# Moving a bookkeeping job of layers 0 and 1 into small parts behind named VectorE copies

## The chip, the cores and the metric

The kernel runs on one NeuronCore of a Trainium2 chip. Its engines each work through their own queue in order: TensorE (PE, matrix products), VectorE (DVE), ScalarE (ACT), GpSimd (POOL) and SyncE (SP, which mostly issues DMAs). The metric is the time of one execution on the device in microseconds.

## The reference

A graph network of four layers over 16 graphs (images, below) of 1024 nodes with 256 features, float32. Each layer adds to x what a graph layer makes of the normalised input:

```python
h = jnp.maximum(_layernorm(x), 0.0);  x = x + layer(h, adj, ...)
# layer 0: h' = h @ W.T + b;  u = adj * exp(e_i + f_j);  a = u / u.sum(2);   a @ h'
# layer 1: (d^-1/2 adj d^-1/2) @ (h @ weight) + bias, d = adj.sum(-1) + 1e-5
# layer 2: node after node, i = 0..1023:
#          x_par = (adj[:, i] / deg)^T h;  a GRU cell of (h_e[i], x_par) gives h[i]
# layer 3: agg = eps*h + adj @ h;  silu(rmsnorm(agg @ W1 + b1)) @ W2 + b2
```

Layer 2 is sequential over nodes. The kernel works it off in groups: within each block of 128 nodes it finds an order in which groups of 16 nodes don't depend on one another, as far as the edges (adj not zero) allow. That order is data, so it is computed in the kernel, by the function `orders`.

## The kernel before

Everything here happens in `layers_0_1` (L247 to L538), about the first 1500 us. A loop over i = 0 to 17 runs layer 0 of image i (`layer_0`) and then layer 1 of image i-1 (`layer_1`), with the preparation of image i+1 (`prepare`: statistics, q in L340, f in L342, then gs in L347) in between. A planner fixes the order of instructions on each engine when the program is built; data waits are added by it.

`sums` computes agg = adj @ h in four parts (two halves of 512 nodes by two halves of the features): eight matmuls each (L309) into one PSUM tile `pa` of two, then a copy to SBUF. Parts with c == 0 are copied by ScalarE (L312), those with c == 1 by VectorE (L314). So each layer of each image has two VectorE copies; counted from 0 over the whole stage, copies 4i-2 and 4i-1 belong to layer 0 of image i, and 4i and 4i+1 to layer 1 of image i-1. After sums come the matmuls with the weights (L379 in layer 0, L410 in layer 1), and pd (L361) takes gs of the next image.

`orders` holds two generators, advanced a part at a time by the loop:

- `places` (L126) reads pieces of adj (`piece`: eight DMAs at L113 and the comparison at L114, into a tile named "ad") and gives every node of a block its place: five small VectorE instructions a node (L135 to L140); then a rank is formed by comparing and reducing 16 columns at once (L149, L151), and a transposition on TensorE (L154). A part comes after each slot of `layer_0`.
- `rest` (L158) makes index tables: L162, 128 instructions, then writes of order_d (SP, L177) and reads of table (GpSimd, L181). It then reads adj again in eight pieces and finds how many rounds each group needs (L195, L196, then L201 to L236, transpositions L222). Its parts come in `layer_1` from i = 9 on, although the planner may place them earlier where nothing holds them.

From i = 9 (`ready`), `put_in_order` permutes what layer 2 will read, images 2k and 2k+1 in iteration 9 + k, image 14 in 16 and 15 in 17: it loads ad (SP, L423, L424), ab (L427) and mostly h (L430), scales ad on GpSimd (L435 to L440), permutes h by matmuls with a one-hot matrix `to` (L448, evacuated by L450 and L452), then ad (L461, L463, evacuated by L468 and L470), and multiplies (L476, L482).

The tiles named "ad" have one buffer together: the pieces of adj in `orders`, the tile `less` of the ranking, and the ad of `put_in_order` use it in turn. The tiles h2 have two buffers, shared by layer 1's output (ScalarE, L301) and by the h that `put_in_order` loads; x (loaded at L322) has three.

Of the kernel before, what the change touches and what calls it, by code (L numbers as in the profile page):

```python
# [2 lines left out]

# [6 lines left out]
F32 = mybir.dt.float32  # L10
AF = mybir.ActivationFunctionType
ALU = mybir.AluOpType
# [4 lines left out]
P = 128  # L17
# [4 lines left out]
S = 16  # L22
# [18 lines left out]
def gnn_stack(ctx: ExitStack, tc: tile.TileContext, a: dict, out: bass.AP):  # L41
# [65 lines left out]
    def orders(pool, psum):  # L107
# [9 lines left out]
        def tile_(name, n=P):  # L117
            return pool.tile([P, n], F32, name="o_" + name)
# [7 lines left out]
        def places():  # L126
            nc.vector.memset(bins, TOP)
            nc.vector.tensor_scalar(open_, step[:, :S], -1.0, TOP - 1, op0=ALU.mult, op1=ALU.add)
            nc.vector.tensor_scalar(below, open_, 1.0, None, op0=ALU.add)
            nc.vector.memset(held, 0.0)  # L130
            for j0 in range(0, P, S):
                nz = piece(j0, ALU.is_equal, 2 * TOP)
                for j in range(j0, j0 + S):
                    mine = bins[:, j : j + 1]
                    nc.vector.scalar_tensor_tensor(fit, below, mine, open_, op0=ALU.is_le, op1=ALU.mult)  # L135
                    nc.vector.tensor_reduce(mine, fit, AX.X, ALU.max)
                    nc.vector.scalar_tensor_tensor(held, open_, mine, held, op0=ALU.is_equal, op1=ALU.add)
                    nc.vector.scalar_tensor_tensor(open_, held, float(S), open_, op0=ALU.is_lt, op1=ALU.mult)
                    if j + 1 < P:
                        nc.vector.scalar_tensor_tensor(bins[:, j + 1 :], nz[:, j - j0, j + 1 :], mine, bins[:, j + 1 :],  # L140
                                                       op0=ALU.add, op1=ALU.min)
                    if j % 8 == 7:
                        yield

            key = tile_("key")
            nc.vector.scalar_tensor_tensor(key, bins, -256.0, step, op0=ALU.mult, op1=ALU.add)
            for i in range(0, P, S):
                less = pool.tile([P, S, P], F32, name="ad")
                nc.vector.tensor_tensor(less, key[:, None].to_broadcast([P, S, P]),  # L149
                                        key[:, i : i + S][:, :, None].to_broadcast([P, S, P]), ALU.is_lt)  # L150
                nc.vector.tensor_reduce(pos[:, i : i + S], less, AX.X, ALU.add)  # L151
                yield
            pt = psum.tile([P, 512], F32, name="pt")
            nc.tensor.transpose(pt[:, :P], pos, ident)  # L154
            nc.vector.tensor_copy(place, pt[:, :P])
            yield

        def rest():  # L158

            node = tile_("key")  # L160
            for p in range(P):
                nc.vector.scalar_tensor_tensor(junk, pos, float(p), step, op0=ALU.is_equal, op1=ALU.mult,  # L162
                                               accum_out=node[:, p : p + 1])
                if p % 32 == 31:
                    yield
# [17 lines left out]
            yield  # L183

            sub = tile_("sub")
            nc.vector.memset(sub, 0.0)
            for s in range(1, NS):
                nc.vector.scalar_tensor_tensor(sub, pos, float(s * S), sub, op0=ALU.is_ge, op1=ALU.add)
            chain = tile_("bins")
            nc.vector.memset(chain, 1.0)  # L190
            for j0 in range(0, P, S):
                nz = piece(j0, ALU.not_equal, 2.0)
                for j in range(j0, min(j0 + S, P - 1)):
                    row = nz[:, j - j0, j + 1 :]
                    nc.vector.scalar_tensor_tensor(row, sub[:, j + 1 :], sub[:, j : j + 1], row, op0=ALU.is_equal, op1=ALU.mult)  # L195
                    nc.vector.scalar_tensor_tensor(chain[:, j + 1 :], row, chain[:, j : j + 1], chain[:, j + 1 :],  # L196
                                                   op0=ALU.mult, op1=ALU.max)
                yield
            top = tile_("top", NS)
            for s in range(NS):  # L200
                nc.vector.scalar_tensor_tensor(junk, sub, float(s), chain, op0=ALU.is_equal, op1=ALU.mult)  # L201
                nc.vector.tensor_reduce(top[:, s : s + 1], junk, AX.X, ALU.max)
# [4 lines left out]
            for s, cuts in CUTS.items():  # L207
                for k, cut in enumerate(cuts):
                    if cut in cuts[:k]:
                        continue  # L210
                    nc.vector.tensor_scalar(junk, pos, float(s * S + cut), None, op0=ALU.is_lt)
                    nc.vector.scalar_tensor_tensor(junk, sub, float(s), junk, op0=ALU.is_equal, op1=ALU.mult)
                    nc.vector.scalar_tensor_tensor(junk, chain, 2.0 ** (k + 1), junk, op0=ALU.is_ge, op1=ALU.mult)
                    nc.vector.tensor_reduce(found, junk, AX.X, ALU.max)
                    nc.vector.tensor_tensor(early[:, s : s + 1], early[:, s : s + 1], found, ALU.max)
# [21 lines left out]
            yield  # L237
        return places(), rest()

# [7 lines left out]
    def layers_0_1():  # L247
        with ExitStack() as st:
# [46 lines left out]
            def normed(x, scale, mv, name, bufs):  # L295
# [6 lines left out]
                return h  # L302

            def sums(at, h, ag):

                def part(n0, c):
# [4 lines left out]
                    if c == 0:  # L311
                        nc.scalar.copy(ag[:, c, n0 : n0 + 512], pa)  # L312
                    else:
                        nc.vector.tensor_copy(ag[:, c, n0 : n0 + 512], pa)  # L314
                return [lambda n0=n0, c=c: part(n0, c) for n0 in (0, 512) for c in range(DC)]
# [39 lines left out]
            def layer_0(b, between):  # L355
# [9 lines left out]
                for part in sums(at[b], q[b], ag):  # L365
                    part()
                    if between:
                        between.pop(0)()
# [32 lines left out]
            def layer_1(b, between):  # L401
                ag = big.tile([P, DC, N], F32, name="ag", bufs=2)
                for part in sums(at[b], h1[b], ag):
                    part()
                    if between:
                        between.pop(0)()
# [85 lines left out]
            when.update({b + 2: (b,) for b in range(14, B)})  # L492
            parts_of_places, parts_of_rest = orders(big, psum)
            load(0)
# [3 lines left out]
            for i in range(B + 2):  # L498
                if i + 1 < B:
                    load(i + 1)  # L500
                jobs = []
                for b in when.get(i, ()):
# [12 lines left out]
                def slot():  # L515
                    for part in slots.pop(0):
                        part()
                    next(parts_of_places, None)
                if i < B:
# [6 lines left out]
                if 0 < i < B - 1:  # L526
# [3 lines left out]
                    between[1] = lambda: (load_half(i + 1), second())  # L530
                if i >= ready:
                    between += [lambda: None] * (4 - len(between))
                    for k in (1, 3):
                        between[k] = lambda part=between[k]: (part(), next(parts_of_rest, None))
                if 1 <= i <= B:
# [734 lines left out]
```

## Time and profile before

| | us |
|---|---|
| median of 3 runs | 4860.91 |
| lowest, highest | 4855.44, 4871.58 |
| the profiled execution | 4861.04 |
| its span | 4858.2 |
| PE busy | 4494.9 (93%) |
| DVE busy | 2303.1 (47%) |
| first copy L314 | starts at 41.77 |
| copy 20, copy 40, copy 63 | start at 457.34, 913.34, 1443.20 |
| first matmul of layer 2 (L749) | 1507.68 |

A line of a view of waits reads: engine, the instruction that waited, the one it waited for, and then us in total, times, and the longest. A line of a timeline reads: start and length in us, engine, line, operation, output and inputs with their sizes, the number of instructions put together, and in brackets the idle time of the engine before, with what ended it. PE matmuls are listed one record for each pass, two to an L309 instruction. Lines are those of the kernel before.

### The profile page before, as it was taken

To read this page: it belongs to the slowest core of one execution; us is meant where nothing else is said; L and a number is where in the kernel's file an instruction comes from. 1 tells how busy PE (TensorE), PEld (TensorE's weight loads), DVE (VectorE), ACT (ScalarE), POOL (GpSimd) and SP (SyncE) were. 2 spreads that over 40 slices of the span, in tenths; PEclk is the share of its full clock that TensorE was granted. 3 is DMA by queue.
4 is the path that set the end of the run, shared out by engine and by line. 5 is a ranking of instruction groups with operands and counts; after the bars stand their busy time and mean duration, and the time that the engine had idled before them with its cause. 6 is when DMAs were issued, how large, how long until landed. Compare 5 with 4: busy or idle time off the path is not lost. (4 is left out here: it accounts for less than half of the span.)

```text
span 4858.2 us, 52472 instructions
## 1 busy us (share of the span) xinstructions
PE 4494.9 (93%) x18199; PEld 3004.6 (62%) x18199; DVE 2303.1 (47%) x6354; ACT 1220.2 (25%) x2629; POOL 1586.6 (33%) x1939
## 2 busy tenths in 40 slices
PE   8998899999997999999999999998899999999999
PEld 4443455555555777777777777776455555555556
DVE  6667854455543444444444444454534344344342
ACT  1211112222212222222322222222223223223232
POOL 3223233343323322332232323331534234243231
PEclk9999999999998999999999999998899999999999
DMA  4333235555537444444344544420422231222100
GB/s 157 113 99 104 88 88 183 194 165 176 184 104 209 149 137 133 149 142 149 115 140 122 157 139 153 142 82 29 169 87 70 78 104 65 91 88 78 70 26 18
DMA packets 530978, 576.61 MB, mean 119 GB/s; under 512 B 42544, under 2 KB 439472, under 8 KB 528304
## 3 DMA queue, kind: packets, MB, share of 16 engines
q1 hardware_dynamic: 499536, 460.27, 30.6%
q0 software_dynamic: 31040, 111.44, 6.4%
q8 instruction: 197, 3.23, 0.3%
q14 instruction: 205, 1.68, 0.1%
HBM read 469.65 MB, written 116.65 MB: 121 GB/s over the span
## 5 line engine op out<-in xcount | busy, mean ns | idle before, releaser
L309 PE MATMUL pa<-at,h 128*128 128x512 f32 x1088 | 497.4, 610 | 32.9 <-DVE ag L314 32.9
L1145 PE MATMUL ph<-ag,w 128*128 128x512 f32 x1024 | 478.3, 609 | 32.7 <-DVE hh L1149 32.4
L1183 PE MATMUL po<-w,hh 128*128 128x256 f32 x2048 | 447.7, 379 | 0.0
L637 PE MATMUL pf<-hb,ab 128*128 128x256 f32 x1568 | 420.6, 387 | 29.0 <-DVE bxt L787 16.2
L1183 PEld LDWEIGHTS po<-w,hh 128*128 128x128 f32 x2048 | 387.8, 190 | 59.3 <-issue 7.9
L309 PE MATMUL pa<-at,q 128*128 128x512 f32 x960 | 424.2, 595 | 0.0
L309 PEld LDWEIGHTS pa<-at,h 128*128 128x128 f32 x1088 | 209.9, 196 | 278.5 <-issue 232.8
L749 PE MATMUL pf<-hs,wx 128*128 128x256 f32 x1536 | 351.1, 383 | 16.6 <-POOL hs L740 14.9
L1145 PEld LDWEIGHTS ph<-ag,w 128*128 128x128 f32 x1024 | 178.6, 189 | 294.0 <-DVE hh L1149 151.4
L1151 POOL TENSOR_TENSOR ss<-ss,sq 128x512 f32<-128x512 f32 x224 | 304.9, 1361 | 118.7 <-ACT sq L1148 114.3
L749 PEld LDWEIGHTS pf<-hs,wx 128*128 128x128 f32 x1536 | 292.1, 192 | 60.1 <-POOL hs L740 16.8
L637 PEld LDWEIGHTS pf<-hb,ab 128*128 128x128 f32 x1568 | 278.2, 192 | 69.5 <-DVE bxt L787 23.4
L309 PEld LDWEIGHTS pa<-at,q 128*128 128x128 f32 x960 | 178.2, 190 | 216.1 <-issue 212.6
L1149 DVE TENSOR_SCALAR hh<-ph,b 128x512 f32<-128x512 f32 x256 | 189.8, 746 | 153.8 <-ACT sq L1148 120.5
L784 PE MATMUL pf<-bd,h 128*128 128x384 f32 (+5 forms) x768 | 214.4, 373 | 51.7 <-DVE bxt L787 26.5
L1034 POOL DMA_INDIRECT hs_d<-h,table x128 | 129.3, 1010 | 365.4 <-ACT gates L757 179.7
L1130 PE MATMUL pa<-bxt,h 128*128 128x512 f32 x512 | 227.9, 597 | 18.6 <-POOL bxt L1112 18.6
L1130 PE MATMUL pa<-at,h 128*128 128x512 f32 x512 | 228.8, 597 | 0.0
L1148 ACT ACTIVATE sq<-ph,b 128x512 f32<-128x512 f32 x224 | 153.6, 686 | 233.6 <-PE ph L1145 188.2
L787 DVE TENSOR_TENSOR bxt<-bxt,pf 128x384 f32<-128x384 f32 (+5 forms) x384 | 141.2, 384 | 149.1 <-PE pf L784 146.6
L1175 ACT ACTIVATE hh<-hh,rw 128x512 f32<-128x512 f32 x256 | 168.4, 712 | 138.5 <-DVE hh L1174 136.5
L754 DVE TENSOR_TENSOR gates<-pf,bias 128x512 f32<-128x512 f32 x128 | 88.4, 691 | 227.3 <-PE pf L749 227.3
(253 smaller groups left out, 7318.6 us busy)
## 6 DMA issues: line engine op xcount, KB each, us to landing
at<-in_adjT SPq DMA_DIRECT2D x64, 1024.0 KB, 7.2
ab<-in_adj SPq DMA_DIRECT2D x128, 512.0 KB, 4.0
bxt<-in_adjT SPq DMA_DIRECT2D x64, 512.0 KB, 5.8
at<-in_adjT SPq DMA_DIRECT2D x64, 512.0 KB, 5.8
ad<-in_adj SPq DMA_DIRECT2D x128, 128.0 KB, 6.0
x_d<-x POOLq DMA_DIRECT2D x16, 1024.0 KB, 5.4
he_d<-h POOLq DMA_DIRECT2D x16, 1024.0 KB, 9.5
heT_d<-hT POOLq DMA_DIRECT2D x16, 1024.0 KB, 4.4
```

The lines of the kernel that those rows point to most:

```text
L309: nc.tensor.matmul(pa, h[:, mt, c * P : (c + 1) * P], at[n0 // 512][:, mt], start=mt == 0, stop=mt == NT - 1)
L637: nc.tensor.matmul(pb, ab[:, jts[k]], hb[:, jts[k]], start=k == 0, stop=k == len(jts) - 1)
L749: nc.tensor.matmul(pg[:, e], wx[:, c, q * D + e * P : q * D + (e + 1) * P], self.hs[:, c], start=c == 0, stop=c == DC - 1)
L784: nc.tensor.matmul(pf, h[:, g, c * P : (c + 1) * P], bd[:, g, b4 : b4 + 4, S : S + far], start=True, stop=True)
L787: return lambda: nc.vector.tensor_add(to, to, pf)
L1130: nc.tensor.matmul(pa, h[b][:, mt, c * P : (c + 1) * P], at[b][n0 // NH][:, mt], start=mt == 0, stop=mt == NT - 1)
L1145: nc.tensor.matmul(ph, w1[:, c, k * P : (k + 1) * P], ag[:, c, n0 : n0 + NH], start=c == 0, stop=c == DC - 1)
L1148: nc.scalar.activation(sq, ph, AF.Square, bias=b1[:, k : k + 1])
L1149: nc.vector.tensor_scalar(hh[:, k], ph, b1[:, k : k + 1], None, op0=ALU.add)
L1151: nc.gpsimd.tensor_tensor(ss, ss, sq, ALU.add)
L1175: nc.scalar.activation(hh[:, k], hh[:, k], AF.Silu, scale=rw[:, k : k + 1])
L1183: nc.tensor.matmul(po, hh[:, c, k * P : (k + 1) * P], w2[:, c], start=c == 0, stop=c == HC - 1)
```

## The change

`places` gives its parts after 4 nodes instead of 8, and ranks 8 columns at once instead of 16, so that L149 and L151 come 16 times at 1024 elements instead of 8 times at 2048. `rest` is split into `tables` (a part after 8 of its 128 instructions instead of 32) and `rounds` (a part after 8 nodes instead of 16; its array `chain` is now called `longest`, and the scratch tile of its end is one named "ad"). All rounds now come directly after all places.

The parts are taken in `layer_0` and `layer_1` after each of the four parts of sums, under `tc.issue_after`, which queues them on VectorE behind the last copy L314. Up to i = 8 these are parts of places and rounds, afterwards parts of tables; what is left of places and rounds at i = 9 is issued there at once. The hooks in `slot` and in `between` from i = 9 on are gone. What is computed stays the same.

```diff
-                    if j % 8 == 7:
+                    if j % 4 == 3:
                         yield
...
-            for i in range(0, P, S):
-                less = pool.tile([P, S, P], F32, name="ad")
-                nc.vector.tensor_tensor(less, key[:, None].to_broadcast([P, S, P]),
-                                        key[:, i : i + S][:, :, None].to_broadcast([P, S, P]), ALU.is_lt)
-                nc.vector.tensor_reduce(pos[:, i : i + S], less, AX.X, ALU.add)
+            yield
+            for i in range(0, P, 8):
+                less = pool.tile([P, 8, P], F32, name="ad")
+                nc.vector.tensor_tensor(less, key[:, None].to_broadcast([P, 8, P]),
+                                        key[:, i : i + 8][:, :, None].to_broadcast([P, 8, P]), ALU.is_lt)
+                nc.vector.tensor_reduce(pos[:, i : i + 8], less, AX.X, ALU.add)
                 yield
...
-        def rest():
+        def tables():
...
-                if p % 32 == 31:
+                if p % 8 == 7:
                     yield
...
+        def rounds():
+
             sub = tile_("sub")
...
-                yield
+                    if j % 8 == 7:
+                        yield
             top = tile_("top", NS)
+            junk = pool.tile([P, P], F32, name="ad")
...
-        return places(), rest()
+        return places(), tables(), rounds()
...
+            taken = []
+
+            def some_of(parts):
+
+                with tc.issue_after(taken[-1].ins):
+                    next(parts, None)
+
             def sums(at, h, ag):
...
-                        nc.vector.tensor_copy(ag[:, c, n0 : n0 + 512], pa)
+                        taken.append(nc.vector.tensor_copy(ag[:, c, n0 : n0 + 512], pa))
...
                 for part in sums(at[b], q[b], ag):
                     part()
+                    if taken:
+                        some_of(places if b < ready else tables)
...
                 for part in sums(at[b], h1[b], ag):
                     part()
+                    some_of(places if b + 1 < ready else tables)
...
-            parts_of_places, parts_of_rest = orders(big, psum)
+            places, tables, rounds = orders(big, psum)
+            places = chain(places, rounds)
...
+                if i == ready:
+                    for _ in places:
+                        pass
...
-                    next(parts_of_places, None)
...
-                if i >= ready:
-                    between += [lambda: None] * (4 - len(between))
-                    for k in (1, 3):
-                        between[k] = lambda part=between[k]: (part(), next(parts_of_rest, None))
```

## The prediction

> **What bounds the kernel now.** I read the page's head first, then the waits of TensorE over layers 0 and 1 (0 to 1470 us; layers 2 and 3 keep their instructions and order), then the timeline of each large wait.
>
> ```profile
> span 4858.2 us, 52472 instructions
> PE 4494.9 (93%) x18199; PEld 3004.6 (62%) x18199; DVE 2303.1 (47%) x6354; ACT 1220.2 (25%) x2629; POOL 1586.6 (33%) x1939
> ```
>
> TensorE is busy 93% of the span, so only its idle time and slowed stretches can be won or lost. Next, who made TensorE wait (us in total, times, longest):
>
> ```profile
> PE pa L309 <- DVE ag L314: 32.9, 12, 4.9
> PE pd L361 <- ACT gs L347: 25.3, 2, 17.4
> PE pmm L410 <- DVE x L411: 14.5, 5, 5.3
> ...
> PE pmm L379 <- DVE deg L375: 3.7, 1, 3.7
> ...
> PE pt L461 <- POOL ad L439: 3.1, 1, 3.1
> ```
>
> The first four trace back to VectorE, which serves the copies of sums late because orders' work stands ahead of them. The 17.4 us one, on VectorE and then on TensorE (start, us, instruction, idle before):
>
> ```profile
> 463.47 2.27 DVE L151 TENSOR_REDUCE o_pos<-ad 128x16 f32<-128x2048 f32 x1
> 465.67 0.34 DVE L340 TENSOR_SCALAR q<-x,mv 128x256 f32<-128x256 f32 x1
> 465.92 2.28 DVE L149 TENSOR_TENSOR ad<-o_key 128x2048 f32<-128x2048 f32 x1
> 468.13 0.94 DVE L342 SCALAR_TENSOR_TENSOR junk<-q,rs,v 128x256 f32<-128x256 f32 x1
> ```
>
> ```profile
> 466.74 1.89 PE L410 MATMUL pmm<-w,ag 128*128 128x256 f32 x8
> 486.07 1.94 PE L361 MATMUL pd<-at,gs 128*32 128x512 f32 x8 [17.44 <-ACT gs L347]
> ```
>
> Each L342 waits behind a compare and a reduction; the last ends at 485.6, so gs and pd come late. A later copy with no orders' work near it, on VectorE and then on TensorE:
>
> ```profile
> 650.42 0.17 DVE L350 TENSOR_TENSOR rg<-rs,gs 128x8 f32<-128x8 f32 x1 [0.37 <-ACT gs L347]
> 650.51 0.68 DVE L314 COPY ag<-pa 128x512 f32<-128x512 f32 x1
> ```
>
> ```profile
> 651.25 7.13 PE L309 MATMUL pa<-at,h 128*128 128x512 f32 x16 [1.44 <-DVE ag L314]
> ```
>
> Here the slack is already spent: eight L340 and L342 fill VectorE from 635.8, and this copy (number 28, counting L314 from 0) holds TensorE for 1.44 us. Whatever is put before it costs its full length.
>
> **What the Trainium skill says.** "TensorE: Matmul & The Clock Gate", its specification table: VectorE's queue is strictly first in, first out. The trace agrees: the copy at 650.51 starts as L350 is out of the way. The same page, Part 1 on the clock gate: an idle window of about 3.4 us drops TensorE to half rate until it has been busy for about as long. Agrees: after the 17.44 us wait, 26 records of L361 took 5.55 us against 2.95 elsewhere, 2.6 more. "VectorE: DVE Perf Modes", the TRN2 errata: a fixed cost per instruction with SBUF operands, 120 cycles beside one per element at 0.96 GHz. For 2048 elements that is 2.26 us, measured 2.28; for 1024, not in the trace of before, I estimate 1.19 us from that page. "Perfetto Trace Analysis", Optimizing Scalar/DVE Operations: breaking up instructions may let work finish sooner; the L342 chain above is such a case.
>
> **The change part by part.** Changes of TensorE's time, plus is slower. The order of instructions on each engine is fixed at build, and I compared it before and after. Up to copy 20 (first five iterations) it is practically the same: a piece of 16 nodes waits for the one ad buffer, not for its place in the queue. Gain there: 0.
>
> A, copies 20 to 27. A turn of the loop above is 463.47 to 469.00 = 5.53 us with one pair L149/L151. Halved blocks take out 2 x 1024 elements / 0.96 GHz = 2.13 us a turn, over five turns 10.7 us. The 128 L162 (pitch 0.334 us, 43 us at 504 to 550) leave this place; with them go waits that the window 457 to 580 and the next give as 7.5 (L309 on copies), 3.7 (deg) and 5.3 (L411), 16.5 together. New: eight half pairs beside later copies, 1.9, and the transpose L154 before copy 25, which waits for the last reduction, 2.8. Sum -22.5; with a little clock -23.
>
> B, rounds moved here from iterations 11 to 17. All pieces stand in a bunch of 31 or 32 L195/L196 right before copies 26, 28, 30 to 40, whatever the finer yields. Before 26 and 30 (in layer_0) VectorE has 7 us of other work in a 24.4 us interval of TensorE's sums and pd, so 8 us fit: 0 (8 each, were that cover gone). Before 28 and 32 the slack is spent: L114 0.7 + 31 x 0.246 (pitch measured for such rows) = 8.3, and for the shorter rows of copy 32 7.2. That is 15.5; two stalls over 3 us each cost 1.5 to 2.7 in the 16 records after them in the other stalls of before, I take 1.3 each since the second is partly absorbed: +18.
>
> C, copies 34 to 37. 48 L162 (16 us) and two pieces. The scheduler puts six of the eight L342 behind copy 36, so the copy is in time; the last copy of the iteration comes some 1.5 us late for L410, less small waits of images that no longer run there: +1. Cover: L342 behind the copy; without it about +8.
>
> D, copies 38 to 42. The pieces and `longest`'s junk hold the one ad buffer until the last L214, about 11 us after copy 40 (some 40 small VectorE instructions of 0.1 to 0.33 us). Only then can image 0's ad be loaded. In the trace of before a load issued at 949.92 is ready for TensorE at 960.9 (landing, L435 1.90, L440 1.68, L439 1.89): 11 us. TensorE meanwhile finishes its part some 4 us after that L214 and then waits about 7. Image 0's transposes take 7.9 us when nothing covers them (1457.4 to 1465.3). On SP, x of image 11 is queued behind image 1's ad, so it goes out about 21 us after image 0's load (11 + 7.9, and two issues) and lands 6.8 us later; statistics about 7, then L340/L342 at 1.6 us for eight: 13, then gs. pd comes 6 to 7 us late again. 7 + 6.5 + two uncovered image chains at 5 to 6 + clock 2.6 = 27, against 2 there before: +25 (10 to 40). Waiting with it on SP: the at loads of that iteration; on VectorE nothing.
>
> E, rest of iteration 11. Images 2 to 5 run in this iteration with one ad buffer: 11 + 7.5 = 18.6 us each, where their places on TensorE are about 15 apart: 3.5 late three times. 16 order_d writes (14 took 17.6 us on SP) and four table reads (2.77 us each on POOL) stand among their loads: mostly in the shadow of that ring. +8 (0 to 28).
>
> F, copies 46 to 61. Before, 357.9 us pass for 320 us of TensorE work at its own pace: 38 lost, 24.0 of it in named waits. In copies 33 to 45, images run without rounds and lose 14.4 in three iterations, 4.8 each. Four such: 19. -19, and a little for the ad buffer no longer shared with L113: -20.
>
> H, the end of layer 1. Before:
>
> ```profile
> 1476.78 3.50 PE L448 MATMUL pt<-to,h 128*128 128x128 f32 x16 [1.70 <-DVE to L432]
> 1481.25 0.44 PE L461 MATMUL pt<-to,ad 128*128 128x128 f32 x2 [0.96 <-POOL ad L439]
> ```
>
> Image 14's ad is loaded only at 1434.66, since L113's last piece held the buffer, and rounds' end stands among L411. From copy 63 (1443.2) to the first L749 (1507.68) are 64.5 us. With the ad buffer free and VectorE clear, L448 of image 15 can end 15.5 us after copy 63 and 25.7 us later comes L749: 41. Of the 23.5, 8.7 is image 14's TensorE work, done earlier and paid there: -15.
>
> Sum: -23 + 18 + 1 + 25 + 8 - 20 - 15 = -6. Span 4858.2 becomes 4852; the profiled run took 4861.04, 2.8 more than its span and level with the median 4860.91, so 4855.
>
> **The rivals.** Faster: the pile-up of D and E costs 8 instead of 33, because image 1's ad and x of image 11 go out while TensorE still has L410. For it: 15 us of other TensorE work lie there. Against: SP's fixed order. -31, so 4830. Decided by x of image 11 having landed within about 15 us of copy 41.
> Slower: SP. If the order_d writes (1.25 us each) delay the ad of images 2 and 3 by up to 20 us, E is 28, and x of image 11 late by 10 more makes D 35: -6 + 20 + 10 = +24, so 4885. For it: each write waits for an earlier transfer. Against: image 1's own chain covers the first eight. Over +0.3% from D + E = 54 on.
> Nothing: what is won up to copy 27 and after 46 is given back exactly by B to E; then 4861. The change doing nothing at all is excluded by the order from copy 20 on.
>
> **How the numbers follow.** 0.3%, 14.6 us, is about what a measurement can tell from no change: below 4846.3 is faster, above 4875.5 slower. The forecast with its own range 4841 to 4869: 0.40 (0.08 of it below 4846.3). Faster rival, 4815 to 4841: 0.28. Slower rival, 4876 to 4900: 0.28. Nothing: 0.04. So faster 0.36, same 0.36, slower 0.28. 4826 to 4890 leaves out about 0.08 and 0.10.
>
> **What would show it.** Right: the 17.4 us wait for gs falls to about 7 and the waits for deg and L411 at 500 to 600 go; L309 waits 9 to 10 us for copies 28 and 32; one group of waits of 20 to 30 us around copies 41 to 43, for ad on POOL and for gs; few waits afterwards; the first L749 some 41 us after copy 63. Wrong: VectorE serves copies 28 and 32 before the bunch (B is 0), or TensorE's idle time at images 0 to 5 is under 10 or over 55 us.

## The result and the profile after

The changed kernel is slower: 4887.26 us, median of 7 runs (4879.17 to 4894.69), against 4863.79 for the kernel before (7 runs, 4855.44 to 4871.58). The ratio is 1.0048, with a 95% interval of 1.0035 to 1.0062. The profiled run took 4883.2 us. Its page begins so:

```profile
span 4881.2 us, 52487 instructions
PE 4501.9 (92%) x18199; PEld 3001.2 (61%) x18199; DVE 2292.3 (47%) x6370; ACT 1219.6 (25%) x2629; POOL 1578.9 (32%) x1939
```

The span is 23.0 us longer, and TensorE's busy time 7.0 us longer with as many instructions. Lines of the kernel after lie 13 to 16 below those of the kernel before: L309 is L322, L314 is L327, L361 is L374, L410 is L426, L448, L461 and L468 are L464, L477 and L484. The view of waits of TensorE, layers 0 and 1 (us in total, times, longest):

```profile
PE pa L322 <- DVE ag L327: 43.4, 12, 9.4
PE pd L374 <- ACT gs L360: 20.3, 3, 8.5
PE pt L477 <- ACT hT L484: 14.8, 8, 6.9
PE pt L477 <- POOL ad L455: 10.6, 2, 8.3
PE pt L464 <- ACT hT L466: 9.5, 2, 6.6
...
PE pmm L426 <- DVE x L427: 7.5, 3, 3.6
```

The waits for x (L411 before, 14.5) and deg (3.7) have shrunk or gone, as the prediction has it. The waits for copies (32.9 before) have grown. Three groups weren't among the large ones: waits of `put_in_order` for hT and for ad.

To see where time went I compared the starts of the VectorE copies L314/L327, counted as in the text above, and took off the time that TensorE's instructions between two of them need (those of the layers by their place in the program, those of `put_in_order` by when they ran) at their clean pace in the trace of before (0.867 us for an L309, 0.432 for an L379 or L410, 0.2275 for an L361, 0.215 for an L371, 0.109 for a transposition, 0.434 and 0.11 for L476 and L482). What is left is lost, by waits or by a slower TensorE. The two kernels don't put the same work of `put_in_order` into a stretch, which this takes out. The stretch from copy 61 to 63, left out here, is -0.2 to 5.2 throughout. In us, in the order in which the kernels come below:

| lost between copies | 0–19 | 19–27 | 27–33 | 33–37 | 37–45 | 45–61 | 63 to layer 2 | layer 2 starts | from there to the end |
|---|---|---|---|---|---|---|---|---|---|
| before | 31.5 | 44.2 | 4.0 | 5.7 | 8.7 | 38.0 | 41.8 | 1507.7 | 3350.5 |
| after | 32.0 | 24.2 | 22.5 | 7.3 | 66.6 | 18.2 | 30.4 | 1534.2 | 3347.0 |
| `halves` | 31.5 | 32.2 | 16.2 | 5.6 | 8.9 | 37.0 | 41.2 | 1505.8 | 3355.0 |
| `halves_sp` | 33.1 | 39.4 | 2.3 | 5.7 | 9.0 | 34.4 | 42.8 | 1499.6 | 3346.3 |
| `rounds_odd` | 30.7 | 21.7 | 8.7 | 4.9 | 87.1 | 18.2 | 30.2 | 1535.0 | 3347.8 |
| `old_rounds` | 32.2 | 22.8 | 2.8 | 5.5 | 45.4 | 44.9 | 39.1 | 1529.1 | 3356.9 |
| `tables_late` | 33.3 | 24.4 | 22.6 | 7.6 | 43.5 | 53.7 | 28.4 | 1545.9 | 3356.4 |
| `three` | 32.2 | 24.1 | 22.5 | 7.3 | 52.1 | 15.4 | 30.0 | 1516.0 | 3338.9 |
| `three_late` | 31.8 | 23.2 | 22.3 | 7.6 | 15.8 | 68.7 | 30.9 | 1533.3 | 3349.2 |
| `tables_sp` | 31.9 | 23.3 | 22.2 | 7.3 | 60.2 | 17.5 | 30.1 | 1525.3 | 3349.6 |
| `three_sp` | 32.2 | 24.1 | 22.5 | 7.3 | 47.3 | 19.1 | 29.7 | 1514.9 | 3337.8 |
| `heT_h2` | 31.2 | 24.0 | 22.5 | 7.3 | 86.7 | 24.5 | 25.5 | 1554.7 | 3358.9 |
| `best2` | 32.3 | 22.6 | 11.9 | 37.3 | 13.0 | 17.0 | 29.0 | 1501.2 | 3345.3 |
| `best3` | 30.3 | 23.8 | 13.2 | 5.1 | 14.8 | 16.8 | 28.8 | 1471.5 | 3352.5 |

After against before: -20.0 from 19 to 27, +18.5 to copy 33, +57.9 from 37 to 45, -19.8 to 61, -11.4 at the end. Layer 2 starts 26.5 later, and 3.5 of that comes back in layers 2 and 3. The loss of 57.9 sits in one place: some 44 us of after's are lost between copies 41 (905.40) and 42 (996.04), all in iteration 11, where images 0 to 5 go through `put_in_order`.

On TensorE the two first stretches look as foretold. Its timeline: the wait for gs halved, the copies 28 and 32 late.

```profile
474.03 6.31 PE L374 MATMUL pd<-at,gs 128*32 128x512 f32 x26 [8.47 <-ACT gs L360]
...
637.85 9.84 PE L322 MATMUL pa<-at,h 128*128 128x512 f32 x16 [9.38 <-DVE ag L327]
...
722.67 10.09 PE L322 MATMUL pa<-at,h 128*128 128x512 f32 x16 [7.50 <-DVE ag L327]
```

The wait for copy 28 was 1.44 us before, and its 16 records then took 7.13. On VectorE the bunch of rounds stands directly ahead of the copy:

```profile
636.89 0.31 DVE L200 SCALAR_TENSOR_TENSOR o_bins<-ad,o_bins 128x97 f32<-128x97 f32 x1
637.12 0.68 DVE L327 COPY ag<-pa 128x512 f32<-128x512 f32 x1
```

The surprise is iteration 11. TensorE's timeline from copy 41 to copy 42, the records with the largest idle time ahead of them:

```profile
932.33 0.47 PE L477 MATMUL pt<-to,ad 128*128 128x128 f32 x1 [6.90 <-ACT hT L484]
...
944.51 3.62 PE L374 MATMUL pd<-at,gs 128*32 128x512 f32 x10 [4.32 <-ACT gs L360]
...
961.63 0.48 PE L477 MATMUL pt<-to,ad 128*128 128x128 f32 x1 [8.33 <-POOL ad L455]
...
988.10 1.97 PE L464 MATMUL pt<-to,h 128*128 128x128 f32 x8 [6.62 <-ACT hT L466]
```

Four stalls, 26.2 us, with TensorE slowed in between: the view by windows gives it a granted clock of 0.80 from 912 to 1005 us, where the whole span has 0.976. What the third stall waits for stands on GpSimd:

```profile
942.24 2.78 POOL L183 DMA_DIRECT2D table<-order_d  x1
945.48 0.57 POOL L501 DMA_DIRECT2D base_d<-bo  x1 [0.47 <-DVE bo L500]
953.94 2.77 POOL L183 DMA_DIRECT2D table<-order_d  x1 [7.89 <-issue]
956.72 1.10 POOL L451 TENSOR_SCALAR_AFFINE_SELECT ad<-ad 128x1024 f32<-128x1024 f32 x1
...
959.68 1.89 POOL L455 TENSOR_TENSOR ad<-ad,dinv 128x1024 f32<-128x1024 f32 x1
```

The ad of image 2 was issued on SP at 934.15, when image 1's last transposition out of that one buffer had just ended (933.67 and 0.42 us), so the order_d writes ahead of it on SP did not hold it up. By the 11 us from issue to ready that step D takes from the trace of before, TensorE could have had it at 945; it has it at 961.6. Behind the first table read GpSimd still sends a write of base_d, at 945.48. Then it does nothing for 7.89 us that the profile explains ("issue") until the second read begins, and ad's scaling stands behind that one. A table read has a record of 2.78 us, but it lands much later:

```profile
DMA to landing us min/median/max: 9.2/10.0/11.3
```

The first read landed 11.3 us after its start, at 953.5, and the second begins at 953.94. The third begins at 963.82 and landed after 9.2 us, at 973.0, and the fourth begins at 973.37. So what a read holds up is the next read, and with it all that stands behind that next read; other instructions follow a read at once, as L451 does here. In `tables_sp`, below, where SP issues the reads, the same scaling begins at 946.66. The writes of heT_d, near_d and next_d stand among the third and fourth read. The tile hT has one buffer, which an image uses twice, for its permuted h and then for its permuted ad, and each of these writes must have landed before TensorE's next transpositions can be put into it. The fourth stall is of this kind: near_d and next_d went out behind the fourth read, at 976.12 and 977.00, and landed after 9.8 and 10.4 us, at 985.9 and 987.4; near_d's of the two images before had taken 6.3 and 5.0.

The trace of before has the same in it, though nothing urgent stood behind it. GpSimd's timeline of before:

```profile
591.70 2.80 POOL L181 DMA_DIRECT2D table<-order_d  x1
602.15 2.75 POOL L181 DMA_DIRECT2D table<-order_d  x1 [7.65 <-issue]
604.89 0.89 POOL L417 DMA_DIRECT2D he_d<-h  x1
612.17 2.76 POOL L181 DMA_DIRECT2D table<-order_d  x1 [6.39 <-issue]
621.61 2.75 POOL L181 DMA_DIRECT2D table<-order_d  x1 [6.68 <-issue]
```

Starts are 9.4 to 10.5 us apart, and the write of he_d (L417) follows the second read at once. The first read landed 10.0 us after its start and the third after 9.1, and the read behind each began 0.3 to 0.4 us later. So four reads in a row take up GpSimd's queue for some 33 us, not 11. rs (L83) behind them was wanted only at 631.99.

The theory for the experiments is this. The 25 us by which D and E together were too small come from the table reads, of which each holds up the next one, and what stands behind that, for about 10 us just where six images need the queue; or, as a rival, from the six images alone, caught up in a row on one ad buffer and one hT buffer, with the rounds' late end in front. A second rival has the rounds themselves as the cause, through B and through when they end.

### The profile page after: what moved, and what is told of

Same layout as the page of the kernel before. It is cut to its first block, busy times and chain, and to the rows that moved or that the text cites. A ratio compares the mean times of both kernels' runs of the same rounds, so it can differ in the third digit from the quotient of the medians.

```text
span 4881.2 us, 52487 instructions
## 1 busy us (share of the span) xinstructions
PE 4501.9 (92%) x18199; PEld 3001.2 (61%) x18199; DVE 2292.3 (47%) x6370; ACT 1219.6 (25%) x2629; POOL 1578.9 (32%) x1939
## 5 line engine op out<-in xcount | busy, mean ns | idle before, releaser
L322 PE MATMUL pa<-at,h 128*128 128x512 f32 x1088 | 503.1, 615 | 43.4 <-DVE ag L327 43.4
L1160 PE MATMUL ph<-ag,w 128*128 128x512 f32 x1024 | 479.3, 610 | 32.3 <-DVE hh L1164 32.1
L322 PE MATMUL pa<-at,q 128*128 128x512 f32 x960 | 428.1, 597 | 0.0
L322 PEld LDWEIGHTS pa<-at,h 128*128 128x128 f32 x1088 | 211.9, 198 | 291.6 <-issue 235.1
L322 PEld LDWEIGHTS pa<-at,q 128*128 128x128 f32 x960 | 178.6, 191 | 213.5 <-issue 209.1
L799 PE MATMUL pf<-bd,h 128*128 128x384 f32 (+5 forms) x768 | 213.5, 372 | 49.5 <-DVE bxt L802 26.5
L1145 PE MATMUL pa<-bxt,h 128*128 128x512 f32 x512 | 227.5, 596 | 18.5 <-POOL bxt L1127 18.5
```

Source lines behind the costliest of these rows:

```text
L322: nc.tensor.matmul(pa, h[:, mt, c * P : (c + 1) * P], at[n0 // 512][:, mt], start=mt == 0, stop=mt == NT - 1)
L799: nc.tensor.matmul(pf, h[:, g, c * P : (c + 1) * P], bd[:, g, b4 : b4 + 4, S : S + far], start=True, stop=True)
L1145: nc.tensor.matmul(pa, h[b][:, mt, c * P : (c + 1) * P], at[b][n0 // NH][:, mt], start=mt == 0, stop=mt == NT - 1)
L1160: nc.tensor.matmul(ph, w1[:, c, k * P : (k + 1) * P], ag[:, c, n0 : n0 + NH], start=c == 0, stop=c == DC - 1)
```

## The experiments

**The smaller comparisons alone.** `halves` changes the kernel before in one place:

```diff
-            for i in range(0, P, S):
-                less = pool.tile([P, S, P], F32, name="ad")
...
+            for i in range(0, P, 8):
+                less = pool.tile([P, 8, P], F32, name="ad")
...
```

> The kernel before with nothing changed but the ranking in sixteen compares and reductions of 1024 elements. My theory of step A: five turns of the loop get 2.13 us shorter, so the wait for gs falls from 17.4 to about 7 us and the time by 10 us, to about 4853; the waits for deg and L411 stay, since the 128 table instructions stay where they are. Rival: the wait was for the whole backlog, and only moves to the next copy: no change, 4863.

4862.32 us against 4860.47 for before, ratio 0.9998 (0.9989 to 1.0007). Step A's first part is real: the stretch 19 to 27 loses 32.2 instead of 44.2, and the wait for gs falls from 17.44 to 8.5 us. But 27 to 33 loses 16.2 instead of 4.0. TensorE's waits there, 580 to 720 us:

```profile
PE pa L309 <- ACT ag L312: 7.0, 1, 7.0
PE pa L309 <- DVE ag L314: 4.2, 1, 4.2
```

The last table read starts 3.9 us later than in the kernel before, while TensorE is 12 us ahead, and this time rs, which is soon wanted, is behind the reads. GpSimd, and then VectorE, which waits for rs with its copies queued behind:

```profile
625.50 2.75 POOL L181 DMA_DIRECT2D table<-order_d  x1 [6.57 <-issue]
...
629.89 1.63 POOL L83 TENSOR_TENSOR rs<-rs_v,mhalf 128x8 f32<-128x8 f32 x1
```

```profile
631.55 0.17 DVE L396 TENSOR_TENSOR rd<-rs,dis 128x8 f32<-128x8 f32 x1 [12.65 <-POOL rs L83]
```

The gain of 12.0 us was given back, 12.2, in the next stretch. The time is the rival's, 4863, but not for the rival's reason, since the wait for gs did not move to the next copy. `halves_sp` adds one edit, the table reads issued by SP:

```diff
-                        nc.gpsimd.dma_start(table[k][:, g].rearrange("p t s -> p (t s)"),
+                        nc.sync.dma_start(table[k][:, g].rearrange("p t s -> p (t s)"),
```

> The kernel before with the sixteen half compares and the table reads issued by SP. In the half-compare kernel the stretch of copies 19 to 27 got 12 us shorter and that of 27 to 33 got 12.2 longer, with an rs on GpSimd 12.65 us late behind the table reads. Theory: with these on SP the 12 us stay won: 4848 to 4852. Rival: VectorE's table instructions, now later, cost the 12 us: 4862.

4852.67 against 4860.38, ratio 0.9982 (0.9973 to 0.9991), just above the range that was expected. The stretch 27 to 33 is back at 2.3, so it was the reads' hold on GpSimd that had taken the gain of `halves`. Layer 2 starts 8.1 us earlier than in the kernel before. But up to copy 27 only 4.8 of the 12.0 is left. On SP the second eight order_d writes now stand behind two reads, and VectorE waits for them, with copy 27 queued behind:

```profile
612.88 0.17 DVE L186 MEMSET o_sub<- 128x128 f32 x1 [14.84 <-DMA order_d<-o_sub]
```

In `halves` this wait is 6.07 us. Copy 27 starts at 615.25 instead of 606.81, and TensorE waits 4.61 us for deg behind it, where `halves` has no wait for deg. So the reads hold up SP too. The second edit was not run alone.

**Rounds.** `rounds_odd` lets the parts of rounds in the kernel after follow only the second and third part of sums, so that none is bunched ahead of the second copy of a layer:

```diff
+                    if b + 1 >= ready or not in_rounds or n in (1, 2):
...
+                    if taken and (b >= ready or not in_rounds or n in (1, 2)):
...
```

> The changed kernel, but parts of rounds are taken only behind the second and third part of sums, so that a piece stands before an odd copy (27, 29, 31, 33), where VectorE has nothing else. Theory (step B): the waits of 9.4 and 7.5 us for copies 28 and 32 go, with their slowed records 19 us, and the rest stays: 4868. Rival: VectorE's total work in these iterations binds, and the same 19 us are lost at other copies: 4887.

4886.59 against 4860.47, ratio 1.0058 (1.004 to 1.0076): no better than after. The time is the rival's, 4887, but the loss is not at other copies of these iterations. B itself goes as it should. From 27 to 33, 8.7 is lost instead of 22.5, and TensorE's waits for these copies, 16.9 us in after, are

```profile
PE pa L325 <- DVE ag L330: 4.9, 2, 3.5
```

But 37 to 45 loses 87.1, 20.5 more than in after. There, 880 to 1090 us:

```profile
PE pt L481 <- ACT hT L488: 24.5, 5, 13.0
PE pt L502 <- DVE hT L490: 7.9, 1, 7.9
```

The third and fourth table read now start at 952.52 and 962.26, and a write of heT_d is issued behind them at 966.70. hT can't be written before it has landed, and the wait of 13.0 us ends at 975.24. So what B costs and what iteration 11 costs are not independent: a gain before it shifts which instruction is behind a read.

`old_rounds` is the reverse: in the kernel after, rounds are given back their place in iterations 11 on.

```diff
-                    if j % 8 == 7:
+                    if j % 16 == 15:
...
-            places = chain(places, rounds)
...
+                if i >= 11:
+                    between += [lambda: None] * (4 - len(between))
+                    for k in (1, 3):
+                        between[k] = lambda part=between[k]: (part(), next(rounds, None))
```

> The changed kernel with places and tables as it has them, but rounds taken two parts an iteration in layer 1 from iteration 11 on, about where the kernel before has them, so that images start in iteration 9, two at a time. If tables alone, among images in iterations 9 to 11, cost what they seemed to (23 us of the 58): between copies 37 and 45 some 30 us are lost, against 8.7 before and 66.6 in the changed kernel, copies 19 to 33 lose 28 (24 and 4), and the time is 4855 to 4870. If rounds in front of the images are the cause of the whole: under 15 us are lost there, 4840 to 4852.

4883.71 against 4862.61, ratio 1.0043 (1.0033 to 1.0052). Without any rounds before it, and with images spaced as before, 37 to 45 still loses 45.4, where before loses 8.7. That is more than either expectation, 30 or under 15, and the time is above both ranges. What is left of the change in these iterations is the tables: their VectorE instructions, the order_d writes and the reads. TensorE's waits from 770 to 1000, and on GpSimd why:

```profile
PE pt L464 <- ACT hT L466: 15.7, 1, 15.7
PE pt L477 <- ACT hT L484: 13.7, 2, 13.1
```

```profile
929.50 2.75 POOL L183 DMA_DIRECT2D table<-order_d  x1 [8.53 <-issue]
...
933.12 0.57 POOL L470 DMA_DIRECT2D heT_d<-hT  x1
```

The read before it stands at 918.16. heT_d goes out 15 us after that, and TensorE's L477 at 944.24 has waited 13.12 us for hT. So rounds in front of the images are not the cause of the whole: 36.7 of the 57.9 us stay without them. And this is F too: with rounds put back, 45 to 61 loses 44.9 instead of 18.2.

**Reads and images, two by two.** In `tables_late`, tables are not made until i is 12. In `three`, six images are not caught up in one iteration: three are taken in each of the iterations 11 to 14. `three_late` has both edits.

```diff
-                        some_of(places if b < ready else tables)
+                        some_of(places if b < ready else tables if b >= 12 else iter(()))
...
-                    some_of(places if b + 1 < ready else tables)
+                    some_of(places if b + 1 < ready else tables if b + 1 >= 12 else iter(()))
```

```diff
-            when = {ready + k: (2 * k, 2 * k + 1) for k in range(7)}
-            when.update({b + 2: (b,) for b in range(14, B)})
+            when = {11 + k: (3 * k, 3 * k + 1, 3 * k + 2) for k in range(4)}
+            when.update({15: (12, 13), 16: (14,), 17: (15,)})
```

> The changed kernel, but tables are taken from iteration 12 on, so that the order_d writes on SP and the table reads on GpSimd are out of iteration 11. If they cause the pile-up there: the wait of 8.3 us for the scaled ad of image 2 and some 5 us behind it go, 4870 to 4875. If the six images in a row cause it by themselves: 4882 to 4890. The table instructions then stand among later images and may cost up to 5 us there in both.

> The changed kernel, but the images are put in order three at a time from iteration 11 on (0 to 2 in 11, 3 to 5 in 12, and so on; 12 and 13 in 15, 14 and 15 as before), so that none waits for rounds to end. If the six images that are caught up in one iteration are the cause: of the 58 us lost more than before between copies 37 and 45 at least 30 go, 4850 to 4860. If the late release of the ad buffer is, by delaying x of image 11: about the same as the changed kernel, 4880 to 4890.

> The changed kernel with images three at a time from iteration 11 and tables from iteration 12: what the late end of rounds costs with neither tables nor six images beside it. Between copies 37 and 45, where the changed kernel loses 66.6 us, the one with images in threes 52.1 and the one with late tables 43.5: if the causes are separate, 25 to 32 us; if images in threes only help because tables are there, 40 to 45. Later the tables cost some 30 us among images, as in the other run with late tables, so the whole is 4870 to 4890.

`tables_late` took 4896.08 against 4860.47, ratio 1.007 (1.0048 to 1.0092); `three` 4857.63 against 4860.47, 0.9998 (0.9987 to 1.001); `three_late` 4882.16 against 4862.61, 1.004 (1.0024 to 1.0055). Lost from copy 37 to 45:

| | tables in iteration 11 | tables later |
|---|---|---|
| six images in iteration 11 | 66.6 (after) | 43.5 |
| three images in iteration 11 | 52.1 | 15.8 |

So the tables as a whole (VectorE instructions, order_d writes and reads) cost 23.1 us beside six images and 36.3 beside three; six images instead of three cost 27.7 without the tables and 14.5 with them. The two overlap: 66.6 is less than 15.8 + 36.3 + 27.7 = 79.8. `three` met its time, 4850 to 4860, but with 14.5 us of the 30 that were expected in this stretch; `tables_late` came out slower than both its ranges, and `three_late` lost less than the 25 to 32 expected. With neither, 15.8 is left, 7.1 above the kernel before. What waits there is the end of rounds, from 854 to 1045 us:

```profile
PE pt L228 <- DVE o_top L208: 6.6, 1, 6.6
PE pt L464 <- ACT hT L466: 2.3, 2, 1.1
```

Moving the tables later doesn't take their price away. `tables_late` loses 53.7 in the stretch 45 to 61, 35.5 more than after, and `three_late` 68.7 there. In `tables_late`, 1060 to 1450 us:

```profile
PE pt L477 <- ACT hT L484: 15.9, 5, 13.2
PE pt L464 <- ACT hT L466: 15.1, 1, 15.1
```

Wherever the reads stand among images of `put_in_order`, hT's writes are behind them.

**The reads on another queue.** `tables_sp` is the kernel after with the edit of `halves_sp`, and `three_sp` is `three` with it.

> The changed kernel, but the four table reads are issued by SP instead of GpSimd, so that nothing on GpSimd stands behind them. Theory: of the 58 us lost between copies 37 and 45 beyond before, the 23 that tables cost there come from GpSimd standing still for the order_d writes, with the scaling of ad and the rs of the normalisation behind it; then 12 to 20 us go, 4867 to 4875. Rival: the DMA transfers themselves or SP's issues cost it: 4882 to 4890.

> The changed kernel with images three at a time from iteration 11 and the table reads on SP. If both causes are separate, their gains add: the 28 us of the one and 12 to 20 of the other, 4838 to 4848. If both remove the same wait: 4855 to 4860.

`tables_sp` took 4876.24 against 4860.38, ratio 1.0029 (1.002 to 1.0038), some 10 us better than after and between the two expectations; `three_sp` 4856.2, ratio 0.9991 (0.9983 to 0.9998), hardly better than `three` and in the range expected if both edits remove the same wait. From copy 37 to 45 `tables_sp` loses 60.2 instead of 66.6, `three_sp` 47.3 instead of 52.1. The Trainium skill says on the page "DMA: Bandwidth & Descriptors", in "Issuing engines are not separate DMA queues", that DMAs of all engines run on the same 16 DMA engines and that issuing from several only saves time on the sequencer. These runs agree that the choice of engine doesn't make most of the cost go: the longest wait of `tables_sp` from 885 to 1000 us is

```profile
PE pt L477 <- POOL ad L455: 13.9, 1, 13.9
```

since ad's load stands on SP, behind the reads (issued at 971.41, right after the second pair). The choice mainly says who is held. In `halves_sp`, where only order_d writes stood behind the reads on SP, layer 2 starts 6.2 us earlier than in `halves`.

**hT's buffer.** `heT_h2` writes heT_d from h2 instead of hT, so that hT comes free earlier. Layer 2 reads other values in this kernel.

```diff
-                        nc.gpsimd.dma_start(heT_d[b], hT)
+                        nc.gpsimd.dma_start(heT_d[b], h2[b].rearrange("p t d -> p (t d)"))
```

> The changed kernel, but the write of heT_d takes its bytes from h2 instead of hT, so that the second use of the one hT buffer need not wait for that write to land; layer 2 then reads other values, with the same instructions and sizes. If the ring over the hT buffer sets the pace of the six images in a row: the waits of TensorE for hT in the first half of an image (10.3 us) go and 8 to 15 us of time with them, 4872 to 4879. If the ad buffer and GpSimd set it: 4883 to 4889.

4914.24 against 4860.38, ratio 1.0098 (1.007 to 1.0126): slower than both expectations. h2 has two buffers itself, which this write now holds, and the waits from 870 to 1110 us are

```profile
PE pt L464 <- ACT hT L466: 27.7, 4, 18.8
PE pt L464 <- DMA h<-he_d: 13.5, 2, 10.0
```

One ring was traded for another, so this run doesn't settle what hT's ring alone costs.

**A version built from these.** `best2` and `best3` keep the places as they are in after, take rounds 16 nodes at a time behind the last part of layer 1's sums from i = 8, let SP issue the table reads, and make tables earlier, in parts that are only queued behind the first VectorE copy of a layer. In `best2` these parts are 16 instructions, in `best3` 21 and a last one of 23, which moves the reads one layer ahead. The core of `best3`, against after:

```diff
+            ranked.append(1)
...
-                if p % 8 == 7:
+                if p % 21 == 20 and p < 105:
                     yield
...
-                        nc.gpsimd.dma_start(table[k][:, g].rearrange("p t s -> p (t s)"),
+                        nc.sync.dma_start(table[k][:, g].rearrange("p t s -> p (t s)"),
...
-                    some_of(places if b + 1 < ready else tables)
+                    if ranked:
+                        next(places, None)
+                        if n in (1, 2):
+                            some_of(tables)
+                    else:
+                        some_of(places)
...
+                if i >= 8:
+                    between += [lambda: None] * (4 - len(between))
+                    for k in (3,):
+                        between[k] = lambda part=between[k]: (part(), next(rounds, None))
```

> What the runs point to: places behind the copies with half compares as in the changed kernel; tables right after them, 32 instructions before each of the copies 27, 29, 31 and 33, where VectorE has nothing else, with their table reads on SP and before any image; rounds one piece an iteration from iteration 8 on in the last part of layer 1's sums, before odd copies; images two at a time from iteration 9 as before. Expected lost between copies: 19 to 27 24 us (44 before), 27 to 33 4 to 6, 33 to 45 15 to 20, 45 to 61 30 to 38, and the end of layer 1 about 10 us shorter, since rounds end earlier: 4830 to 4842. If tables' transfers cost the same wherever they are: 4850 to 4860.

> The previous version of this kind with tables in parts of 21 instead of 16, so that all 128 stand before the copies 27, 29 and 31, and order_d and the table reads are through one layer earlier, before SP has an image's h to load. There a wait of 22.0 us for that h stood, in a stretch (copies 33 to 37) that lost 37.3 us against 5.7 before. If the table reads on SP held it up: the stretch loses 6 to 15 us, the one before it (11.9) up to 8 more, since the reads now meet the at loads there, and the time is 4823 to 4835. If the h was late for another reason: 4845 to 4850.

`best2` took 4848.4 against 4862.61, ratio 0.9973 (0.9964 to 0.9981). The time is between the two expectations. Its stretch 33 to 37 loses 37.3 us, because the reads fall in front of an image once more: on TensorE, and on SP ahead of it,

```profile
762.96 1.97 PE L476 MATMUL pt<-to,h 128*128 128x128 f32 x8 [22.03 <-DMA h<-he_d]
```

```profile
725.32 7.75 SPq L186 DMA_DIRECT2D table<-order_d  x2
733.12 9.65 SPq L182 DMA_DIRECT2D order_d<-o_sub  x8
...
744.57 6.07 SPq L186 DMA_DIRECT2D table<-order_d  x2
750.73 6.63 SPq L458 DMA_DIRECT2D h<-he_d  x1
```

`best3` took 4815.24 us, median of 4 runs (4812.86 to 4825.97), against 4859.51: ratio 0.9906 (0.989 to 0.9923), faster than the 4823 to 4835 that were expected. Its profiled run is the slowest of the four. It loses 5.1 from 33 to 37, and its page says

```profile
span 4824.0 us, 52489 instructions
PE 4488.7 (93%) x18199; PEld 3002.0 (62%) x18199; DVE 2304.1 (48%) x6370; ACT 1219.5 (25%) x2629; POOL 1569.0 (33%) x1935
```

Layer 2 starts at 1471.5, 36.2 us before that of the kernel before. The only edit between `best2` and `best3` is the size of the parts of tables, which moves their last instructions, the order_d writes and the reads ahead by a layer, and the stretch 33 to 37 loses 32.2 us less for it: the clearest measure of what tables cost in the wrong place.

## Why the prediction was wrong

The forecast was 4855, a span 6 us shorter. The span came out 23.0 longer. By its own steps:

- **A**, -23 forecast, -20.0 measured (44.2 to 24.2). The wait for gs fell from 17.44 to 8.47, "about 7" was said, and the transposition (L156 after) waits 6.46 instead of 2.8: 3.7 us are lost by that one. The shorter compare and reduction took 1.21 us each instead of 2.28, so a turn of the loop has 2.1 us less to do, as forecast.
- **B**, +18 forecast, +18.5 measured. Waits of 9.38 and 7.50 at copies 28 and 32, and 2.7 and 3.0 us lost to a slower TensorE behind them, where "9 to 10" and 1.3 for each were said. `rounds_odd` shows that it is the bunch: without it 13.8 of these go.
- **C**, +1 forecast, +1.6 measured.
- **D and E** are where the prediction failed: +33 forecast for both, +57.9 measured. D's chain came about much as it was worked out. Image 0's ad went out on SP at 894.15, x of image 11 at 920.47, 26 us later where 21 was said, and the wait for gs at 944.51 is 4.32 where 6.5 was said. The step that was wrong is the sentence in E on 16 order_d writes and four table reads "(2.77 us each on POOL)", "mostly in the shadow of that ring". It priced a DMA issue by the length of its record. The Trainium skill warns of this on the page "Perfetto Trace Analysis", in "Per-instruction lifecycle": the profiled window of a DMA instruction leaves the data's movement out. The trace agrees (2.78 us of record, 9.2 to 11.3 to landing), and shows more: a second read begins only when the first has landed, and the queue on which ad's scaling, rs and hT's writes stand waits with it. Two of the four stalls of iteration 11 lead back to reads, and E had nothing for them: the 8.33 us to the held queue, the 6.62 us to writes of hT that landed late behind the fourth read (that the read made them late is likely, but not shown apart). The table by reads and images puts the tables at 23.1 us beside six images, nearly all of the 24.9 that were missing. Without them the stretch loses 34.8 us more than in the kernel before (`tables_late`, 43.5 against 8.7), near to the 33 of D and E together. How much of the 23.1 is the reads, and how much the order_d writes and VectorE's part, no run separates: with the reads on SP 6.4 of it go, but there they hold up ad's load. E had no term for hT's one buffer either, which six images in a row use twelve times; the waits of 6.90 and 6.62 are for hT. And E's own working, 3.5 us late three times, is 10.5, not 8.
- **F**, -20 forecast, -19.8 measured; `old_rounds` undoes it, to 44.9.
- **H**, -15 forecast, -11.4 measured: from copy 63 to layer 2 it takes 44.4 us, not 41.

So A and H were 3.0 and 3.6 too large, D and E 24.9 too small, and layers 2 and 3 gave 3.5 back: -6 + 3.0 + 3.6 + 24.9 - 3.5 is 22, beside 23.0 measured. The slower rival came closest in number, 4885, and wanted D + E = 63, but its mechanism was SP: order_d writes that hold up ad. That isn't what the trace shows. Ad of image 2 was issued 22.6 us before GpSimd began to scale it, and what held it was GpSimd's queue, where the scaling stood behind the second read. Only where the reads were put on SP (`tables_sp`) did SP hold ad.

The bound named for being wrong was an idle time of TensorE "at images 0 to 5" over 55 us. The five largest groups of waits from 880 to 1080 us are 40.3 together; the loss of 66.6 holds the slower TensorE between them too, which that bound left out. The sign named for being right, waits of 20 to 30 us around copies 41 to 43 for ad and for gs, came as well: the four stalls are 26.2 us. So neither sign told the forecast from what happened.

What stays open: why a read of table does not begin before the one ahead of it has landed, since the profile says only "issue"; whether reads set apart from one another would cost less, which no run tried; and how much of the six images' 27.7 us is hT's ring and how much the one ad buffer, as `heT_h2` didn't separate them.

## What to carry to other kernels

Don't price a DMA by its record. See in the trace when it lands, and whether the next one of its kind on that queue begins before that: idle time marked "issue" ahead of the next one is the sign that it doesn't, and then everything behind that one waits too. When DMAs are moved, list what stands behind them at the new place on the queue that issues them and who waits for that: here a gain of 12 us was given back in full because one small GpSimd instruction that was soon wanted came to stand behind four reads, and moving tables and reads by one layer was worth 32. When a gain and a loss share a queue, measure both edits alone and together, since they don't add.

## What the runs showed of the hardware that was not expected

- A read of table, a DMA of 32 KB that GpSimd issues, has a record of 2.75 to 2.81 us and lands in 9.0 to 11.3 us in the traces of before, after, `old_rounds` and `three`. Where the landing is on record and the next read was ready, the next read began 0.3 to 0.4 us after it, 9.4 to 11.7 us after the start of the first; instructions of other kinds followed a read at once. When SP issues two in a row, the first has a record of 0.38 us and the second of 7.3 or 5.6 (`best2`), and what follows on SP is slow as well: eight order_d writes have a record of 9.65 us together, in after of 3.67.
- After 9.38 us of idle time, TensorE took 9.84 us for 16 records that take 7.13 elsewhere, 2.7 more, and after 7.50 it took 10.09, 3.0 more. After 17.44 us it was 2.6 (the prediction's figure). The loss did not grow with the length of the wait. The view by windows gives a granted clock of 0.50 from 637.85 to 643 us and 0.92 from 643 to 645, so half the rate lasted some 5 us here, longer than the 3.4 that the prediction had.
- From the start of layer 2 to the end, the same instructions took 3337.8 to 3358.9 us in the profiles of these fourteen kernels. This spread of 21 us is as large as most steps of the prediction, so the edits of layers 0 and 1 were judged stretch by stretch. The spans alone would credit `three` with 26.3 us against after; layer 2 starts 18.2 us earlier in it, and the other 8.1 lie in layers that the edit doesn't touch.
